# Decoder layer on one core: values of four heads and eight token tiles by seven-for-eight products applied twice, weights fetched in sets through one ring of blocks

## The chip, the cores and the metric

The kernel runs on one core of a Trainium2 chip. The metric is the device time of one execution in microseconds (us). Five engines work side by side, each through its own instructions in order: TensorE (PE, matrix products; PEld is its loading of weights), VectorE (DVE), ScalarE (ACT), GpSimd (POOL) and SyncE (SP, which issues most of the DMAs). An engine waits for another by semaphores. A product is summed in PSUM and must be read out of there by DVE or ACT before its place can be used again.

## What is computed

A decoder layer in float32 over 32 sequences of 64 tokens, width 512: 2048 tokens. The part that matters here is the first block, self-attention with 32 heads of 128 dimensions:

```python
q = (hidden_states @ Wq + bq).reshape(b, n, H, HD)
k = (hidden_states @ Wk + bk).reshape(b, n, H, HD)
v = (hidden_states @ Wv + bv).reshape(b, n, H, HD)
q = rmsnorm(q, gq)
k = rmsnorm(k, gk)
scores = jnp.einsum('bnhd,bmhd->bhnm', q, k) * scale
attn = jax.nn.softmax(scores.astype(jnp.float32), axis=-1).astype(q.dtype)
out = jnp.einsum('bhnm,bmhd->bnhd', attn, v).reshape(b, n, H * HD)
return out @ Wo + bo
...
x = x + _L0_attn_ref(_layernorm(x, axis=-1), ...)
x = x + _L0_xattn_ref(_layernorm(x, axis=-1), ctx_1024, ...)
x = x + _L0_ffn_ref(_layernorm(x, axis=-1), ...)
```

Attention is within a sequence of 64 tokens (b = 32, n = 64). A cross-attention and a mixture of experts follow; the change touches them only through the memory that the attention frees.

## The kernel before, in words

**Tiles.** The 2048 tokens are 16 tiles of 128. The attention runs over the tiles in two halves of eight (`half` 0 and 1), and in each half over 16 groups of two heads (`hg` 0 to 15). One half with one group is called a window here. The eight tiles of a half lie as seven blocks `x1` to `x7` (`halves_x`): the left factors of a seven-for-eight product, in which a 2 x 2 product of matrices is made of seven products of sums of the quarters instead of eight products of the quarters. Such a scheme pays for the product it saves with additions: of the left factors once, of the right factors (the weights), and of the results, which are added to several places when they are read out of PSUM.

**Queries and keys** of windows 1 to 15 use the scheme twice, one inside the other (`Window.outer`, `inner_x`, `Weights.inner`): 49 products of 128 by 128 by 256 (L736) in place of 64. `Window.project` walks four stages n = 0 to 3, which carry outer products (1, 5), (2, 6), (7, 3) and (4) alone. Each stage has four slots m = 0 to 3; stages 0 to 2 have 14 matmuls, stage 3 has 7. Results leave PSUM by `keep` (L747 on DVE, L757 on DVE and L750 on ACT with the bias, in stage 0) and `end` (L760 on DVE). PSUM has three such banks (`ps_a`), and a slot's first product often goes to the bank that the slot before it filled, with `first=False`: it adds to what is there, so it has to wait until `keep` has read that.

**Values** use the scheme once (`HeadGroup.values`, L440): seven steps for each four tiles (a unit, two to a window), each step of four matmuls of 128 by 128 by 128, read out in 128 x 256 pieces by ACT (L456) and DVE (L460). A window has 14 slots in which one value step is put between the products of queries and keys (`Window.v`, and the `plan` in `double`): four in stage 0, three in stage 1, four in stage 2, three in stage 3.

**What else a window carries** is the attention of earlier units: `scale` (POOL L616, ACT L618) at slots (1, 0) and (2, 0), `scores` (L628) and `mix` (L665) at (1, 3) and at the end, the softmax (DVE L281 to L289, ACT L284, POOL L290), the transposition of the probabilities (`turn_probabilities`, L273, L651) at (1, 1) and (3, 2). Within stages 2 and 3, `add` (L816) adds parts of the queries and keys to each other, unit 0 on POOL and unit 1 on DVE, both operands in SBUF; `squares` (ACT L407) squares the results, and at the window's end `sums_of_squares` (L872) sums the squares on PE.

**Weights.** `Weights` holds one group's queries, keys and values in one tile of four blocks of 128 x 2048 (tag "four", two of them). Six DMAs of 256 KB fetch it (L108). POOL makes the sums for the outer scheme (`sums`, L133, four of 128 x 768 a window) and for the inner one (`more_sums`, L163 to L166, four of 128 x 512 and four of 128 x 384).

**Order.** The order on PE, DVE, ACT and POOL within the attention is the program's order (`manual_schedule`); each engine's queue is then run in order. The order of SP's DMAs is chosen by a scheduler. After the attention comes the output projection with `wo` (`wo_sums`, `first_out`, `strassen_out`, L930), and then cross-attention and experts, interleaved.

Of the kernel before, what the change touches and what calls it, by code (L numbers as in the profile page):

```python
# [13 lines left out]
P = 128  # L14
# [4 lines left out]
HG = 2  # L19
# [22 lines left out]
def decoder_layer(  # L42
# [28 lines left out]
    blocks = ctx.enter_context(tc.tile_pool(name="blocks", bufs=7))  # L71
# [11 lines left out]
    def four_blocks(name):  # L83
        four = blocks.tile([P, 4 * BLK], F32, tag="four", name=name, bufs=2)
        return [four[:, bass.ts(i, BLK)] for i in range(4)]
# [5 lines left out]
    class Weights:  # L91
# [3 lines left out]


        def __init__(self, name, hg, queues, between=None):

            self.hg = hg
            all_ = blocks.tile([P, 4 * BLK], F32, tag="four", name=f"w_{name}", bufs=2)  # L100
            n = 2 * W3

            self.w = all_[:, 0 : 4 * n].rearrange(
                "p (k c j h d) -> p k c j h d", k=2, c=2, h=HG, j=3
            )
            for k in range(2):
                for j, src in enumerate((wq, wk, wv)):
                    queues[j].dma_start(  # L108
                        out=self.w[:, k, :, j, :, :].rearrange("p c h d -> p c (h d)"),
                        in_=src[2 * k * P : (2 * k + 2) * P, bass.ts(hg, HW)].rearrange(  # L110
                            "(c p) f -> p c f", p=P
                        ),
                    )
                if between and k == 0:
                    between()
            self.t = all_[:, 4 * n : 7 * n].rearrange("p (i c j d) -> p i c j d", i=3, c=2, j=3)
            b11, b12, b21, b22 = (self.w[:, k, :, :, h, :] for k in range(2) for h in range(HG))
            t1, t2, t4 = (self.t[:, i, :, :, :] for i in range(3))

            self.right = {1: b11, 2: b21, 3: b22, 4: t4, 5: t1, 6: t2, 7: b12}  # L120
            self.more = all_[:, 7 * n : 7 * n + 21 * HD].rearrange(
                "p (i o d) -> p i o d", i=3, o=7
            )
# [7 lines left out]
        def sums(self, engine):  # L131
            def subtract(on, out, a, b):
                on.tensor_tensor(  # L133
                    *(it.rearrange("p c j d -> p (c j) d") for it in (out, a, b)), ALU.subtract
                )

            b11, b12, b21, b22 = (self.w[:, k, :, :, h, :] for k in range(2) for h in range(HG))
            t1, t2, t4 = (self.t[:, i, :, :, :] for i in range(3))
            subtract(engine, t1, b12, b11)
            subtract(engine, t2, b22, t1)  # L140
            yield
            subtract(nc.gpsimd, b12, b22, b12)
            subtract(nc.gpsimd, t4, b21, t2)
            yield

        def more_sums(self):

            for b, of in (
                (self.w.rearrange("p k c j h d -> p c j k h d"), slice(0, 4)),
                (self.t.rearrange("p i c j d -> p c j i d"), slice(4, 7)),  # L150
            ):

                def part(c, j):
                    it = b[:, c, j]
                    return it

                def more(i):
                    it = self.more[:, i, of, :]
                    return it.rearrange("p (k h) d -> p k h d", k=2) if of.start == 0 else it

                b11, b12, b21, b22 = (part(c, j) for c in range(2) for j in range(2))
                t1, t2, t4 = (more(i) for i in range(3))
                nc.gpsimd.tensor_tensor(t1, b12, b11, ALU.subtract)  # L163
                nc.gpsimd.tensor_tensor(t2, b22, t1, ALU.subtract)
                nc.gpsimd.tensor_tensor(t4, b21, t2, ALU.subtract)
                nc.gpsimd.tensor_tensor(b12, b22, b12, ALU.subtract)  # L166
                yield
            self.inner = {}
            for n, o in enumerate((1, 7, 2, 3, 5, 6, 4)):
                r = self.right[o]  # L170
                t1, t2, t4 = (self.more[:, i, n, :] for i in range(3))
                self.inner[o] = {
                    1: r[:, 0, 0, :],
                    2: r[:, 1, 0, :],
                    3: r[:, 1, 1, :],
                    4: t4,
                    5: t1,
                    6: t2,
                    7: r[:, 0, 1, :],
                }  # L180


# [125 lines left out]
    class AttentionInput:  # L308
# [3 lines left out]
        def __init__(self, pair, beside=False, first_alone=False):  # L312

            self.pair = pair
            places = [None, None]
            if beside:
                both = work.tile([P, 2, 2, QT], F32, tag="rsb", name=f"xs{pair}", bufs=2)
                places = [both[:, i, :, :].rearrange("p h n -> p (h n)") for i in range(2)]
            self.xs, self.pt = [], []
            for place in places[0 : 1 if first_alone else 2]:  # L320
                self.load(place)
# [64 lines left out]

    inner_x = {}
# [22 lines left out]
    class HeadGroup:  # L410
# [7 lines left out]
        def __init__(self, hg, quad, w):  # L418
            self.hg, self.quad, self.w, self.name = hg, quad, w, f"{hg}_{quad}"

            self.qk, self.v, self.gains = {}, {}, None
# [9 lines left out]
        def values(self):  # L431


            name, right, left = self.name, self.w.right, quads[self.quad]

            def product(i, to, first=True):

                for j in range(2):
                    for c in range(2):
# [3 lines left out]
                            right[i][:, c, 2, :],  # L443
# [8 lines left out]
            def keep(h, ab, what):  # L452
                self.v[h, ab] = work.tile(
                    [P, 2, HD], F32, tag="v", name=f"v{h}{ab}_{name}", bufs=18
                )
# [247 lines left out]
    class Window:  # L703
# [5 lines left out]
        def __init__(self, units, w, half):  # L709
            self.units, self.w, self.half = units, w, half  # L710
            self.name = f"w{w.hg}_{half}"
            self.values = [it for unit in units for it in [unit.values()] * 7]
# [8 lines left out]
        def v(self):  # L721
            next(self.values.pop(0))
# [5 lines left out]
        def outer(self, os, banks, to, add=None, bias=None):  # L728

            name = f"{os[0]}_{self.name}"  # L730
            n = len(os)
            pa, pb, pc = (it[:, 0:n, :] for it in banks)

            def product(i, bank, first=True):
                for s, o in enumerate(os):
                    nc.tensor.matmul(  # L736
                        bank[:, s, :],
                        self.w.inner[o][i],
# [53 lines left out]
        def project(self, plan):  # L792

            units, hg = self.units, self.w.hg
# [51 lines left out]
            for n, args in enumerate(  # L846
# [10 lines left out]
                for m, _ in enumerate(self.outer(args[0], turned, *args[1:])):  # L857
# [37 lines left out]


# [46 lines left out]
    def wo_sums(b, places):  # L943
# [11 lines left out]
        def make():  # L955
# [10 lines left out]
            for half in range(2):  # L966
                t4.append(block(f"wo_t4{half}").rearrange("p (g f) -> p g f", f=DH))
# [3 lines left out]
        return {1: b11, 2: b21, 3: b22, 4: t4, 5: t1, 6: t2, 7: b12}, make()  # L971
# [516 lines left out]
    b2 = work.tile([2 * NHEAD, HD], F32, tag="v", name="b2", bufs=18)  # L1488
# [7 lines left out]
    coming.extend(AttentionInput(pair, True) for pair in (2, 3))  # L1496
# [97 lines left out]

    groups = [(hg, half) for half in range(2) for hg in range(NHG)]

    def prepare(n):
        if n + 1 < len(groups):
            hg, half = groups[n + 1]
# [305 lines left out]
```

## Time and profile before

| | us |
|---|---|
| median of three runs (1852.62 to 1854.78) | 1854.5 |
| the execution that was profiled | 1854.15 |
| its span, first to last instruction | 1852.4 |
| one window, from stage 0 of one to stage 0 of the next (463.15 to 504.30) | 41.15 |
| from 50 to 1340, about the 30 windows with doubled products | 1290 |
| after 1340: output projection, cross-attention, experts | 512 |

| engine | busy us (share of span) | in the window 463.15 to 504.30 |
|---|---|---|
| PE | 1838.6 (99%) | 41.15 |
| DVE | 1156.5 (62%) | 26.64 |
| ACT | 721.0 (39%) | 19.22 |
| POOL | 860.2 (46%) | 23.51 |

The granted clock of TensorE is 0.999 of full speed. The DMAs moved 165.01 MB; the main queue's packets took 27.8% of the time of the 16 DMA engines. The busy time of PE overlaps at its ends: eight records of L440 have a busy time of 1.05 us, and the next group begins 0.89 us after they began. A float32 matmul of the program is two records in the trace, so the 1470 matmuls of L736 are its 2940 records.

### The profile page before, as it was taken

The numbers are of one execution on the slowest core, as the hardware profiler recorded it, in microseconds if no ns is written. First come the engines' busy times: TensorE is split into PE (matmuls) and PEld (weight loads), VectorE is DVE, ScalarE is ACT, GpSimd is POOL, SyncE is SP. The second block draws the span as 40 slices with busy tenths as digits, with TensorE's granted clock in tenths as the row PEclk, the third lists the DMA queues.
The fourth block names the chain that finished last, engine by engine and source line by source line (L and its number), as shares of the span: only waits on it lengthen the run. The fifth ranks groups of instructions, "written<-read, shape, count | busy, mean of one in ns | idle before, by whom it ended". The sixth has DMA issues, their size and how long they took to land.

```text
span 1852.4 us, 40846 instructions
## 1 busy us (share of the span) xinstructions
PE 1838.6 (99%) x16892; PEld 1605.2 (87%) x16892; DVE 1156.5 (62%) x2044; ACT 721.0 (39%) x1651; POOL 860.2 (46%) x786
## 2 busy tenths in 40 slices
PE   9999999999999999999999999999999999999998
PEld 8889988998899888889888998898888788888876
DVE  7766667676666657666666666666684444544455
ACT  3344445445444443444444444444412112211222
POOL 4855655565556428655556665565132221212120
PEclk9999999999999999999999999999999999999999
DMA  3133323323332232222233222222835221223100
GB/s 127 54 105 99 84 81 93 92 76 88 90 87 73 82 104 70 70 81 70 72 103 87 76 70 70 81 70 73 273 119 183 94 103 61 89 100 110 53 26 24
DMA packets 225099, 165.01 MB, mean 89 GB/s; under 512 B 77776, under 2 KB 204304, under 8 KB 220816
## 3 DMA queue, kind: packets, MB, share of 16 engines
q1 hardware_dynamic: 217808, 156.30, 27.8%
q10 hardware_dynamic: 7104, 6.10, 1.0%
q8 instruction: 133, 2.18, 0.5%
q14 instruction: 54, 0.44, 0.1%
HBM read 121.98 MB, written 40.37 MB: 88 GB/s over the span
## 4 chain that ended last, share of the span: by engine, by line
PE 97%; DVE 2%; DMA 1%; ACT 0%; issue 0%; POOL 0%; SPq 0%; DVEq 0%; POOLq 0%; ACTq 0%
PE p_w L736 35%; PE py L930 21%; PE va L440 12%; PE vb L440 9%; PE s L628 4%; PE o L665 4%; PE ms_w L872 3%; PE pt_p L273 2%; PE pa L498 1%; PE e_x L1159 1%; PE py_x L1175 1%; PE pt_x L273 1%; PE py_x L1170 1%; PE pb L498 1%; PE pm_f L1302 0%; PE pt_f L273 0%
## 5 line engine op out<-in xcount | busy, mean ns | idle before, releaser
L736 PE MATMUL p_w<-x,w 128*128 128x256 f32 x2940 | 720.6, 382 | 2.2 <-DVE qk L747 1.5
L736 PEld LDWEIGHTS p_w<-x,w 128*128 128x128 f32 x2940 | 521.5, 190 | 58.2 <-issue 2.0
L747 DVE TENSOR_TENSOR qk<-p_w,qk 128x512 f32<-128x512 f32 x360 | 212.9, 599 | 145.1 <-PE p_w L736 144.0
L760 DVE TENSOR_TENSOR qk<-p_w,qk 128x512 f32<-128x512 f32 x360 | 222.2, 623 | 101.7 <-PE p_w L736 98.4
L290 POOL TENSOR_TENSOR prob<-prob,inv 128x512 f32<-128x512 f32 x64 | 72.4, 1131 | 454.7 <-PE va L440 237.4
L440 PEld LDWEIGHTS va<-w,x 128*128 128x128 f32 x2048 | 268.5, 192 | 13.0
L440 PE MATMUL va<-w,x 128*128 128x128 f32 x2048 | 269.9, 275 | 0.0
L456 ACT COPY v<-va 128x256 f32<-128x256 f32 x256 | 96.6, 377 | 401.9 <-PE va L440 401.9
L407 ACT ACTIVATE sq<-qk 128x512 f32<-128x512 f32 x256 | 161.3, 631 | 176.4 <-DVE qk L760 57.8
L133 POOL TENSOR_TENSOR w<-w 128x768 f32<-128x768 f32 x124 | 225.0, 1825 | 9.2 <-DMA w<-in_wv_dram 6.9
L930 PE MATMUL py<-wo,a 128*128 128x256 f32 x992 | 227.0, 382 | 0.0
L930 PEld LDWEIGHTS py<-wo,a 128*128 128x128 f32 x992 | 183.8, 190 | 33.4 <-issue 8.9
L440 PEld LDWEIGHTS vb<-w,x 128*128 128x128 f32 x1536 | 201.4, 192 | 9.7
L440 PE MATMUL vb<-w,x 128*128 128x128 f32 x1536 | 202.4, 275 | 0.0
L930 PE MATMUL py<-wo_t,a 128*128 128x256 f32 x672 | 154.9, 381 | 0.0
L930 PEld LDWEIGHTS py<-wo_t,a 128*128 128x128 f32 x672 | 124.7, 190 | 18.9 <-issue 2.4
L1054 POOL TENSOR_TENSOR x<-x,p 128x256 f32<-128x256 f32 x42 | 40.7, 988 | 164.2 <-ACT p L1107 73.9
L460 DVE TENSOR_TENSOR v<-vb,v 128x256 f32<-128x256 f32 x192 | 81.0, 422 | 49.0 <-PE vb L440 27.9
L816 POOL TENSOR_TENSOR qk<-qk 128x256 f32<-128x256 f32 x120 | 90.7, 756 | 28.0 <-DVE qk L760 23.3
L680 ACT ACTIVATE ot<-o,bvt 128x256 f32<-128x256 f32 x256 | 99.4, 469 | 2.2 <-PE o L665 2.2
L281 DVE TENSOR_TENSOR prob<-s,g_w 128x512 f32<-128x512 f32 x60 | 41.5, 691 | 85.9 <-PE s L628 81.3
L284 ACT ACTIVATE prob<-prob 128x512 f32<-128x512 f32 x64 | 40.4, 631 | 128.7 <-DVE prob L283 128.7
(254 smaller groups left out, 2290.3 us busy)
## 6 DMA issues: line engine op xcount, KB each, us to landing
mixed<-ot SPq DMA_DIRECT2D x64, 512.0 KB
a<-mixed SPq DMA_DIRECT2D x32, 1024.0 KB
w<-in_wq_dram SPq DMA_DIRECT2D x64, 256.0 KB
w<-in_wk_dram SPq DMA_DIRECT2D x62, 256.0 KB
w<-in_wv_dram SPq DMA_DIRECT2D x62, 256.0 KB
g_w<-row_w SPq DMA_DIRECT2D x120, 128.0 KB
x<-in_x_dram SPq DMA_DIRECT2D x20, 256.0 KB
wo<-in_wo_dram SPq DMA_DIRECT2D x4, 1024.0 KB
```

The source lines that it names most:

```text
L133: on.tensor_tensor(*(it.rearrange("p c j d -> p (c j) d") for it in (out, a, b)), ALU.subtract)
L407: nc.scalar.activation(sq, of, AF.Square)
L440: nc.tensor.matmul(to[:, j, :], left[i][:, c, j, :], right[i][:, c, 2, :], start=first and j == 0 and c == 0, stop=c == 1, skip_group_chec ...
L456: nc.scalar.copy(self.v[h, ab], what)
L460: nc.vector.tensor_tensor(it, what, it, ALU.add)
L628: nc.tensor.matmul(s[h * SEQ : (h + 1) * SEQ, i, b, :], qk[:, 0, tok], qk[:, 1, tok], start=True, stop=True,)
L680: nc.scalar.activation(ot[:, h, :, b * SEQ : (b + 1) * SEQ], o[b][:, h, :, :], AF.Identity, bias=bvt[:, hg * HG + h : hg * HG + h + 1],)
L736: nc.tensor.matmul(bank[:, s, :], self.w.inner[o][i], inner_x[self.half, o][i], start=first and s == 0, stop=True, skip_group_check=True,)
L747: nc.vector.tensor_tensor(to(t, j), bank, add(t, j), ALU.add)
L760: nc.vector.tensor_tensor(to(t, j), bank, to(t, j), ALU.add)
L816: on.tensor_tensor(to, to, what, ALU.add)
L930: nc.tensor.matmul(py, a[:, g, :], b[g // KH][:, g % KH, :], start=n == 0 and g == 0, stop=n == last and g == NHG - 1,)
```

## The change

Windows 0 and 1 of each half make their values as before. From window 2 on, the values of two windows (four heads) and of all eight tiles of the half are made together, by seven-for-eight products applied twice (`ValueGroup`): 49 products of 128 by 128 by 256, each as two matmuls of 128 columns, 98 matmuls for two windows where there were 112. They form 25 steps in four sets: 14 steps in the even window's slots, 11 in the odd window's, whose last three slots (stage 3) have none. A step of sets 0 to 2 has four matmuls as before, and its result is 128 x 512 for each read-out; set 3's steps have four matmuls for two products (one in the last), and its read-outs are 128 x 256. In set 0, four of seven read-outs are copies on ACT, all others are additions on DVE. Set 2 adds eight `join` additions of 128 x 256 with both operands in SBUF, four on POOL (tiles t = 0) and four on DVE (t = 1).

The weights come as `WeightSet`s, one for each stage, four for the queries and keys of a window and four for the values of two windows. Each takes one block of a single ring of 13 blocks, which also holds the seven blocks of the half's tiles; the ring of seven and the two tiles of four blocks go. Sets 2 and 3 fetch one column half of the weights again instead of reading it from sets 0 and 1. POOL makes one or two sums of 128 x 512 for the outer scheme of a set (`outer_sums`) and four of 128 x 256 (in set 3 of 128 x 128) for the inner one (`inner_sums`).

The first windows' `Weights` take four blocks of the ring, and 12 DMAs in place of six. `wo`'s first loads move from the start of the last window to slots (1, 0) and (2, 0). One sum of `wo` (`wo_t4`) lies in a buffer of the attention and is made a second time behind it (`make_again`). Some buffers change their tag.

```diff
-    blocks = ctx.enter_context(tc.tile_pool(name="blocks", bufs=7))
+    blocks = ctx.enter_context(tc.tile_pool(name="blocks", bufs=13))
...
     def four_blocks(name):
-        four = blocks.tile([P, 4 * BLK], F32, tag="four", name=name, bufs=2)
-        return [four[:, bass.ts(i, BLK)] for i in range(4)]
+        return [block(f"{name}{i}") for i in range(4)]
...
+    class WeightSet:
+        def __init__(self, n, name, sources, width, base):
+            self.n = n
+            it = block(f"ws{n}_{name}")
+            self.raw = it[:, 0 : 8 * HD].rearrange("p (o c f) -> p o c f", o=2, c=2)
+            self.more = it[:, 8 * HD : 16 * HD].rearrange("p (e o d) -> p e o d", e=4, o=2)
+            for j, src in enumerate(sources):
+                to = self.raw[:, :, :, j * width : (j + 1) * width]
+                if n < 2:
+                    for c in range(2):
+                        nc.sync.dma_start(
+                            out=to[:, :, c],
+                            in_=src[bass.ts(2 * n + c, P), base : base + 2 * width].rearrange(
+                                "p (o f) -> p o f", o=2
+                            ),
+                        )
+                else:
+                    base_ = base + (width if n == 2 else 0)
+                    nc.sync.dma_start(
+                        out=to.rearrange("p o c f -> p (o c) f"),
+                        in_=src[:, base_ : base_ + width].rearrange("(k p) f -> p k f", p=P),
+                    )
+            self.slots = slice(1, 2) if n == 3 else slice(0, 2)
+
+        def outer_sums(self, before):
...
+            a, b = (self.raw[:, o] for o in range(2))
+            if self.n == 0:
+                subtract(b, b, a)
+            elif self.n == 1:
+                subtract(b, b, before.raw[:, 1])
+            elif self.n == 2:
+                subtract(a, b, a)
+            else:
+                subtract(b, b, before.raw[:, 0])
+                subtract(b, b, a)
+
+        def inner_sums(self, part):
...
+            for out, a, b in ((t1, b12, b11), (t2, b22, t1), (t4, b21, t2), (t7, b22, b12))[
+                2 * part : 2 * part + 2
+            ]:
+                nc.gpsimd.tensor_tensor(out, a, b, ALU.subtract)
...
+    class ValueGroup:
...
+        def outer(self, n, os, to, add):
...
+            def product(i, bank, first=True):
+                for s, o in enumerate(os):
+                    x = inner_x[self.half, o][i]
+                    for t in range(2):
+                        nc.tensor.matmul(
+                            bank[:, s, bass.ts(t, HD)],
+                            x[:, bass.ts(t, HD)],
+                            right[s][i],
+                            start=first and s == 0 and t == 0,
+                            stop=True,
+                            skip_group_check=True,
+                        )
+
+            def keep(bank, t, j):
+                if add is None:
+                    nc.scalar.copy(to(t, j), bank)
+                else:
+                    nc.vector.tensor_tensor(to(t, j), bank, add(t, j), ALU.add)
+
+            def end(bank, t, j):
+                nc.vector.tensor_tensor(to(t, j), bank, to(t, j), ALU.add)
+
+            def join(t, j):
+                if n == 2:
+                    on = nc.vector if t else nc.gpsimd
...
+                    on.tensor_tensor(p2, p2, p3, ALU.add)
+                    on.tensor_tensor(p3, p3, p1, ALU.add)
+
+            short = n == 3
+            product(1, pa)
+            keep(pa, 0, 0)
+            if not short:
+                yield
+            product(2, pb)
+            end(pb, 0, 0)
+            join(0, 0)
+            yield
...
-                (0, 3): [lambda n=n: sums_of_next(n), lambda: make(1)],
-                (1, 0): [lambda: make(1)],
-                (1, 3): [lambda: make(1)],
-                (3, 0): [lambda: make(2)],
...
+            places = [(n, k) for k in range(4)] + [(n + 1, k) for k in range(2)]
+            for k in range(4):
+                for at in places[k + 2 if (hg, k) != (1, 0) else 1 : k + 3]:
+                    if at[0] == n or hg < NHG - 1:
+                        also(k, 0, lambda at=at: load_qk(*at))
+                at = places[k + 1]
+                if at[0] == n or hg < NHG - 1:
+                    also(k, 1, lambda at=at: sums_of(qk_sets, *at))
+                    also(k, 2, lambda at=at: qk_sets[at].inner_sums(1))
+            for k in range(2):
+                at = (half, hg // 2, 2 * (hg % 2) + k + 1)
+                if at[2] == 4:
+                    at = (half, at[1] + 1, 0)
+                if 0 < at[1] < NHG // 2:
+                    also(2 * k, 0, lambda at=at: load_v(*at))
+                    also(2 * k, 3, lambda at=at: sums_of(v_sets, *at))
+                    also(2 * k + 1, 1, lambda at=at: v_sets[at].inner_sums(1))
...
+            if hg == 1:
+                values = [it for unit in units for it in [unit.values()] * 7]
+            elif hg % 2 == 0:
+                steps = group.steps()
+                values = [steps] * 14
+            else:
+                values = [steps] * 11
+            double(Window(units, n, half, values), more)
...
+    make_again()
```

## The prediction

> **What bounds the kernel now.** First the page: busy times and slices.
>
> ```profile
> span 1852.4 us, 40846 instructions
> PE 1838.6 (99%) x16892; PEld 1605.2 (87%) x16892; DVE 1156.5 (62%) x2044; ACT 721.0 (39%) x1651; POOL 860.2 (46%) x786
> ...
> DVE  7766667676666657666666666666684444544455
> ...
> POOL 4855655565556428655556665565132221212120
> ```
>
> PE never rests, and DVE and POOL have 30 to 45% left in the first 28 slices, which are the attention. That is a mean; the change loads particular stages. So next, the busy time in stretches: one whole window, then stages 2 and 3 of the window before it (columns: us; PE, PEld, DVE, ACT, POOL busy; clock; DMA share; GB/s).
>
> ```profile
> 463.15:504.30 41.15, 41.15 (x449) 36.93 (x443) 26.64 (x47) 19.22 (x38) 23.51 (x20) 1.00 0.28 79
> 443.16:452.88 9.72, 9.72 (x66) 9.00 (x61) 7.53 (x14) 4.40 (x9) 5.05 (x7) 1.00 0.18 56
> 452.88:459.11 6.23, 6.23 (x44) 5.59 (x42) 5.27 (x11) 3.52 (x7) 4.22 (x4) 1.00 0.02 4
> ```
>
> DVE is busy 12.8 of the 15.95 us of these two stages (80%): the room there is 3.2 us, not 14. Third, the timeline, for prices: PE's slots, then DVE beside POOL in stage 3.
>
> ```profile
> 406.48 1.05 PE L440 MATMUL vb<-w,x 128*128 128x128 f32 x8
> 407.37 1.89 PE L736 MATMUL p_w<-x,w 128*128 128x256 f32 x8
> 409.10 1.05 PE L440 MATMUL va<-w,x 128*128 128x128 f32 x8
> 409.99 1.03 PE L736 MATMUL p_w<-x,w 128*128 128x256 f32 x4
> 410.85 1.05 PE L440 MATMUL vb<-w,x 128*128 128x128 f32 x8
> ```
>
> From start to start a value step takes 0.89 us (407.37 - 406.48), a slot's products 1.73 us in stages 0 to 2 and 0.86 in stage 3.
>
> ```profile
> 493.94 0.41 DVE L816 TENSOR_TENSOR qk<-qk 128x256 f32<-128x256 f32 x1
> ...
> 495.29 1.00 POOL L164 TENSOR_TENSOR w<-w 128x384 f32<-128x384 f32 x1
> 495.59 0.98 DVE L816 TENSOR_TENSOR qk<-qk 128x256 f32<-128x256 f32 x1
> 496.37 1.06 POOL L165 TENSOR_TENSOR w<-w 128x384 f32<-128x384 f32 x1
> ...
> 496.83 0.74 DVE L747 TENSOR_TENSOR qk<-p_w,qk 128x256 f32<-128x256 f32 x2
> 497.39 0.99 POOL L166 TENSOR_TENSOR w<-w 128x384 f32<-128x384 f32 x1
> 497.49 1.18 DVE L816 TENSOR_TENSOR qk<-qk 128x256 f32<-128x256 f32 x1
> ```
>
> The same addition of two SBUF operands takes 0.41 us alone and 0.98 or 1.18 beside POOL: each ends about 0.3 us after the POOL instruction that was running when it began. Over its 120 instances (page: 85.2 us) the mean is 0.71. Two PSUM read-outs in a row take 0.74 together, so the second costs 0.33.
>
> **What the change removes on PE.** 14 fewer value matmuls in each of 14 pairs of windows: 196. At 0.886 / 4 = 0.2215 us each that is 43.4 us, or 3.1 a pair. By steps: the even window keeps 14 full steps, so its 41.14 us; the odd one has 7 full and 7 half steps, 41.14 - 12.40 + 9.30 = 38.04 us. The whole saving is in the odd window, and in its stage 3 no value step is left between the products.
>
> **What it adds on DVE.** Prices: 128 x 512 from PSUM 0.64 in a row (443.69 to 444.33, L283 then L747; 0.69 for one alone), 128 x 256 0.33, a softmax operation that depends on the one before 0.72. An addition with both operands in SBUF costs c. The odd window's stages 1 to 3: queries and keys 7 x 0.64 + 7 x 0.64 + 7 x 0.33 = 11.27; values, three read-outs of set 2 and seven of set 3, 1.92 + 2.31 = 4.23; softmax 3 x 0.72 + 0.89 = 3.05; four joins and four additions L816, 8c. Together D = 18.55 + 8c. PE's own work from stage 1 to the end of the sums of squares: 7 x 0.866 + 3 x 0.886 + 0.44 + 2.17 = 11.33 (the 0.44 a transposition, the 2.17 scores and mixture), then 7 x 0.866 + 7 x 0.443 = 9.16, then 7 x 0.433 + 0.44 = 3.47, then 1.86: 25.82.
>
> DVE's queue is tied to PE's at both ends: it can begin 1.07 us after stage 1 (a product and the 0.2 us to the read-out), it waits about 0.2 us for PE in six places (1.2), and behind its last read-out come ACT's square, 0.63, and the last of the sums of squares, some 0.35. So the stretch lasts at least D + 3.25, and PE stalls D - 22.6 = 8c - 4.0. At c = 0.41 that is nothing, at the mean of 0.71 it is 1.7, at the longest row (1.19) 5.5. I take c from POOL's load. Now POOL is busy 57% of a window and c is 0.41 + 0.30, so a busy POOL costs 0.53; at 90%, worked out next, c = 0.41 + 0.9 x 0.53 = 0.89, and the stall is 3.1 us. It eats the saving.
>
> The place where it is felt: a slot's first product adds to a bank that `keep` of the slot before must have read (L747). The value step between gave `keep` 0.89 us. In stage 3 of the odd window it is gone, so two products of 0.43 us stand between a product and the next on its bank, against 0.2 + 0.42 and what is queued before it on DVE: L816, joins, value read-outs. Behind a late L816 wait ACT's squares, and behind them PE's sums of squares.
>
> The even window: stages 2 and 3 get seven value read-outs of 0.64 where DVE had three of 0.42, +3.2, and four L816 at 0.89 instead of 0.75, +0.6, on 12.8: 16.6 against 15.95. I take 0.7 us of stall (0 if slack in the banks holds it, 1.5 if each lateness meets PE).
>
> **What it adds on POOL.** Prices: 128 x 512 1.28 (L163), 128 x 256 0.73 (L816 on POOL, its median), 128 x 128 0.46 by the same slope. A window's four sets of queries and keys: 5 x 1.28 + 12 x 0.73 + 4 x 0.46 = 17.0; values half of as much, 8.5; additions 2.9, gains and softmax 4.2: 32.6 us in the even window and, with four joins, 35.5 in the odd one, against 23.5 now. That is 79% and 93% of 41.14 and 38.04. [...] I add nothing for POOL on top (0 to 3 us a pair): its late weight sums are due a stage later, about three slots of 2.6 us.
>
> [...]
>
> **DMA and SP.** A window's weights grow from 1.5 to 3 MB (sets 2 and 3 fetch a column half again) and rows from 1 KB to 512 B for queries and keys. Weights are 1.5 of 79 GB/s x 41.15 us = 3.25 MB, so 0.13 of the 0.28 DMA share. Priced by bytes the share becomes 0.41, by packets (1536 to some 5000) about 0.58: hidden either way. SP issues about 15 weight DMAs a window, not 6, at 0.46 us: 6.9 us of 41. Each waits for a block of the ring; 13 less 7 leaves six, and behind it on SP stand the rows that the gains come from. The list of the built program has the loads one to two stages ahead of their sums, so I price this wait at nothing; if that cover fails, see the last rival.
>
> **Small terms.** At the start ACT issues eight weight DMAs instead of four before its first layernorm operation, which now begins (5.28) just as the last issue ends (5.18): 4 x 0.45 = +1.8. In windows 3, 5, 7, 9 of half 0 a normalization (0.6 us on DVE) falls in stage 1 of the odd window: +2.4 (0 if hidden). `make_again`, two DVE operations of about 2.28 us, is covered by a DVE that is 40 to 50% busy after 1340; without that cover +4.6. `wo`'s later loads have three stages left: nothing; one late stage would be 10.
>
> **Sum.** A pair: -3.1 + 3.1 + 0.7 = +0.7; 14 pairs +10; with 1.8 and 2.4: +14 on the profiled 1854.15 gives 1868. That execution lies 0.35 below the median, inside the runs' spread of 2.2, so I leave it. Within 0.2% (3.7 us) a measurement cannot tell a change here.
>
> **The rivals.**
> 1. *PE stays the bound, faster.* c stays at 0.71 and slack in the banks holds the even windows: -3.1 + 1.7 = -1.4 a pair, -20 + 4: 1838; with no stall at all, 1811 + 4. For it: the trace has no PE wait above 2.2 us in all of L736, though DVE is 80% full there. Against it: DVE's sums above and the rows beside POOL. Range 1811 to 1850.
> 2. *No change*: stalls a little under my sum, 1851 to 1858.
> 3. *Late weights, slower.* From the point where a set's load waits for its ring block until less than a stage (10 us) is left, POOL's queue stands at the first sum for the DMA, and PE after it. Now such a wait (POOL L133, 6.9 us in three) is 2.3 us; one in each of 28 windows gives 64, so 1920. Against it: loads come early in the list.
>
> **How the numbers follow.** My case 0.57, rival 1 0.30, rival 2 0.05, rival 3 0.08. Faster 0.30, same 0.05, slower 0.65. My case alone spans 1858 (c = 0.8) to 1905 (c about 1.1, even windows 1.1 late: -3.1 + 4.8 + 1.1 = +2.8 a pair, 39 + 4 = 1897, and some POOL on top). The range cuts the lower part of rival 1 and the top of my case and rival 3: 1828 to 1905.
>
> **What would show it.** Right: value matmuls 1372 plus 224 for 1792; even windows near 42 us and odd ones near 41 to 42, not 38; PE idle before the products of stages 2 and 3 and the sums of squares, released by DVE's read-outs and ACT's squares; DVE near 30 us a window, POOL above 32, and the two-SBUF additions near 0.9. Wrong: odd windows of 38 to 39 us with PE as full as now (rival 1), or PE and POOL idle behind weight DMAs (rival 3).

## The result and the profile after

The changed kernel takes 1885.68 us (median of four, 1885.16 to 1886.6) against 1854.64 of the kernel before in the same session: ratio 1.0167, 95% interval 1.0149 to 1.0184. It is 31 us slower; the forecast was 13.4 us slower. The profiled execution has a span of 1884.9 us against 1852.4, so 32.5 us are to be found in it. First the page of the changed kernel: busy times, then the chain of waits by engine, then three groups (columns as in the prediction's page: busy us, mean ns, idle before, what ended it).

```profile
span 1884.9 us, 41677 instructions
PE 1831.8 (97%) x16500; PEld 1569.0 (83%) x16500; DVE 1298.2 (69%) x2270; ACT 664.9 (35%) x1483; POOL 1170.1 (62%) x1414
...
PE 77%; POOL 11%; DVE 9%; issue 3%; DMA 0%; ACT 0%; POOLq 0%; SPq 0%; DVEq 0%; ACTq 0%
...
L768 PE MATMUL p_w<-x,ws_q 128*128 128x256 f32 x2940 | 731.9, 386 | 34.2 <-POOL ws_q L199 20.0
...
L437 ACT ACTIVATE sq<-qk 128x512 f32<-128x512 f32 x256 | 157.5, 629 | 362.6 <-POOL qk L848 219.3
...
L318 POOL TENSOR_TENSOR prob<-prob,inv 128x512 f32<-128x512 f32 x64 | 72.3, 1129 | 209.0 <-DVE inv L317 143.0
```

PE has 392 records fewer (196 matmuls), but the chain that ended last, 97% PE before, now runs 11% through POOL and 9% through DVE. The products (L768) waited 20.0 us for POOL's inner weight sums (L199). POOL itself is busy only 62%, and its softmax multiplication (L318) was preceded by 209 us of idle POOL, 143 of them ended by DVE's reciprocal (L317). POOL idles and is waited for at once; that points at the order of its work rather than at its amount, which e5 tests.

Next an even and an odd window (columns: us; PE, PEld, DVE, ACT, POOL busy; clock; DMA share; GB/s).

```profile
439.37:480.96 41.59, 41.52 (x449) 37.06 (x443) 30.09 (x51) 18.44 (x34) 33.30 (x41) 1.00 0.41 115
480.96:522.68 41.72, 39.59 (x421) 33.67 (x415) 33.71 (x59) 15.98 (x30) 35.51 (x44) 1.00 0.42 116
```

Both are longer than the 41.15 of before (41.14 between sums of squares); the odd one should have lost 3.1 us of PE work, and its PE is busy 1.9 us less than the even one's, but it stands. Its PE pauses, and beside them POOL's queue in the same stretch (timelines: start, duration, then the idle time before and its releaser in brackets):

```profile
512.15 0.71 PE L978 MATMUL va<-ws_v,x 128*128 128x128 f32 x4 [0.31 <-DVE v L994]
...
514.25 1.13 PE L768 MATMUL p_w<-x,ws_q 128*128 128x256 f32 x4 [0.18 <-POOL ws_q L199]
516.63 1.13 PE L768 MATMUL p_w<-x,ws_q 128*128 128x256 f32 x4 [1.25 <-POOL ws_q L199]
```

```profile
503.25 1.86 POOL L199 TENSOR_TENSOR ws_q<-ws_q 128x256 f32<-128x256 f32 x2
506.72 1.04 POOL L318 TENSOR_TENSOR prob<-prob,inv 128x512 f32<-128x512 f32 x1 [1.61 <-ACT ot L710]
507.72 1.04 POOL L646 TENSOR_TENSOR g_w<-g_w,rq 128x512 f32<-128x512 f32 x1
508.72 1.53 POOL L848 TENSOR_TENSOR qk<-qk 128x256 f32<-128x256 f32 x2
510.21 1.27 POOL L175 TENSOR_TENSOR ws_q<-ws_q,ws_q 128x512 f32<-128x512 f32 x1
511.55 1.33 POOL L175 TENSOR_TENSOR ws_q<-ws_q 128x512 f32<-128x512 f32 x1
512.97 1.24 POOL L199 TENSOR_TENSOR ws_q<-ws_q 128x128 f32<-128x128 f32 x2
514.16 1.59 POOL L848 TENSOR_TENSOR qk<-qk 128x256 f32<-128x256 f32 x2
515.72 0.86 POOL L199 TENSOR_TENSOR ws_q<-ws_q 128x128 f32<-128x128 f32 x2
```

POOL stops at 505.11 with the multiplication at the head of its queue. Behind it stand the gains (L646), the additions (L848) and the sums of set 3 (L175, L199), whose last ends at 516.58; PE's product starts at 516.63. The odd row names ACT's L710 as the releaser, which ended at 506.70; DVE's reciprocal (L317), which the multiplication reads, had ended at 506.55, so without L710 it would have stood there only 0.15 us less. Set 3's weights are not the reason: SP had issued their last fetch by 477.98, and POOL's sums of them begin at 510.21 without a wait for a DMA. In the even window the same head waits longer:

```profile
464.24 1.04 POOL L318 TENSOR_TENSOR prob<-prob,inv 128x512 f32<-128x512 f32 x1 [6.53 <-DVE inv L317]
```

Taking the period from one window's sums of squares to the next gives the whole account (us of span, changed minus before):

| place | forecast | measured |
|---|---|---|
| start, to the first sums of squares | +1.8 | +6.4 |
| the first doubled window (hg = 1) of each half | 0 | +2.9 and +3.3 |
| 14 pairs of windows (even 41.67, odd 41.64) | +10 | +14.7 |
| normalizations beside odd windows 3, 5, 7, 9 of half 0 (42.5) | +2.4 | +3.5 |
| single units | 0 | -0.3 |
| everything behind the last window | 0 | +2.0 |
| sum | +14 | +32.5 |

The first doubled windows have the longest pauses of PE in the windows. It waits there for parts of the left factors (`x`, L426) that POOL makes behind set 3's sums, and works on at a clock of 0.50 (last section), so that eight matmuls of L473 took 1.77 us, not 1.05:

```profile
777.13 1.13 PE L768 MATMUL p_w<-x,ws_q 128*128 128x256 f32 x4 [2.18 <-POOL x L426]
778.10 1.77 PE L473 MATMUL va<-wv,x 128*128 128x128 f32 x8
```

What the 2.0 us behind the last window are isn't settled; e5 gets 0.8 of them back.

### The profile page after: what moved, and what is told of

It is laid out like the page before. It is cut to its first block, busy times and chain, and to the rows that moved or that the text cites. A ratio compares the mean times of both kernels' runs of the same rounds, so it can differ in the third digit from the quotient of the medians.

```text
span 1884.9 us, 41677 instructions
## 1 busy us (share of the span) xinstructions
PE 1831.8 (97%) x16500; PEld 1569.0 (83%) x16500; DVE 1298.2 (69%) x2270; ACT 664.9 (35%) x1483; POOL 1170.1 (62%) x1414
## 4 chain that ended last, share of the span: by engine, by line
PE 77%; POOL 11%; DVE 9%; issue 3%; DMA 0%; ACT 0%; POOLq 0%; SPq 0%; DVEq 0%; ACTq 0%
PE p_w L768 24%; PE py L1070 21%; PE va L978 6%; POOL ws_q L175 4%; PE vb L978 4%; PE s L658 4%; POOL qk L848 3%; PE ms_w L904 3%; PE o L695 3%; DVE qk L779 3%; POOL ws_q L199 2%; PE pa L528 2%; POOL g_w L646 2%; PE va L473 1%; PE pt_p L301 1%
## 5 line engine op out<-in xcount | busy, mean ns | idle before, releaser
L768 PE MATMUL p_w<-x,ws_q 128*128 128x256 f32 x2940 | 731.9, 386 | 34.2 <-POOL ws_q L199 20.0
L768 PEld LDWEIGHTS p_w<-x,ws_q 128*128 128x128 f32 x2940 | 521.9, 191 | 113.1 <-POOL ws_q L199 31.3
L199 POOL TENSOR_TENSOR ws_q<-ws_q 128x256 f32<-128x256 f32 x480 | 337.1, 712 | 21.0
L437 ACT ACTIVATE sq<-qk 128x512 f32<-128x512 f32 x256 | 157.5, 629 | 362.6 <-POOL qk L848 219.3
L779 DVE TENSOR_TENSOR qk<-p_w,qk 128x512 f32<-128x512 f32 x360 | 210.6, 596 | 83.6 <-PE p_w L768 72.8
L978 PEld LDWEIGHTS va<-ws_v,x 128*128 128x128 f32 x1568 | 209.0, 191 | 21.0 <-DVE v L994 10.0
L978 PE MATMUL va<-ws_v,x 128*128 128x128 f32 x1568 | 212.6, 276 | 4.4 <-DVE v L994 4.4
L318 POOL TENSOR_TENSOR prob<-prob,inv 128x512 f32<-128x512 f32 x64 | 72.3, 1129 | 209.0 <-DVE inv L317 143.0
L978 PEld LDWEIGHTS vb<-ws_v,x 128*128 128x128 f32 x1176 | 154.5, 192 | 6.5
L978 PE MATMUL vb<-ws_v,x 128*128 128x128 f32 x1176 | 158.5, 275 | 0.0
L199 POOL TENSOR_TENSOR ws_v<-ws_v 128x256 f32<-128x256 f32 (+1 forms) x224 | 147.4, 668 | 8.8
L175 POOL TENSOR_TENSOR ws_q<-ws_q 128x512 f32<-128x512 f32 x90 | 116.8, 1298 | 2.4
L710 ACT ACTIVATE ot<-o,bvt 128x256 f32<-128x256 f32 x256 | 99.2, 469 | 2.2 <-PE o L695 2.2
L848 POOL TENSOR_TENSOR qk<-qk 128x256 f32<-128x256 f32 x120 | 89.1, 742 | 5.3 <-DVE qk L792 0.6
```

Source lines behind the costliest of these rows:

```text
L175: nc.gpsimd.tensor_tensor(*(it.rearrange("p c f -> p (c f)") for it in (out, a, b)), ALU.subtract)
L199: nc.gpsimd.tensor_tensor(out, a, b, ALU.subtract)
L318: nc.gpsimd.tensor_tensor(prob, prob, _bc(inv, k), ALU.mult)
L437: nc.scalar.activation(sq, of, AF.Square)
L710: nc.scalar.activation(ot[:, h, :, b * SEQ : (b + 1) * SEQ], o[b][:, h, :, :], AF.Identity, bias=bvt[:, hg * HG + h : hg * HG + h + 1],)
L768: nc.tensor.matmul(bank[:, s, :], right[s][i], inner_x[self.half, o][i], start=first and s == 0, stop=True, skip_group_check=True,)
```

## The experiments

All edits are made on the changed kernel unless said otherwise. e1 to e9 were run once each, e11 four times, e10 and e12 ten times; the kernel before took 1852.6 to 1857.7 us beside them, so small differences between single runs are read from the windows, which agree much more closely (the 14 doubled windows behind the first of half 0 take 584.80 us in the changed kernel and 584.85 in e3). The letters in the expectations: P is POOL's order (something early in its queue waits, and weight sums stand behind it), D is VectorE's load as the prediction had it, C the amount of POOL's work wherever it stands, S the start. An edit shifts the lines below it: L850 in e1 and e11 is L848 of the changed kernel, L770 is L768, L781 is L779.

**e1_late: the multiplication later in POOL's queue.**

```diff
         nc.vector.reciprocal(inv, sums)
+        yield
         nc.gpsimd.tensor_tensor(prob, prob, _bc(inv, k), ALU.mult)
...
-            waiting.append(lambda: next(it, None))
+            step = lambda: next(it, None)
+            waiting.extend([step] + [lambda: None] * 3 + [step])
```

> The changed kernel, with the softmax's multiplication on POOL issued about two slots later, behind the additions L848 and the first sums of the next weight set; nothing else is changed. POOL's order (theory P): POOL stands at that multiplication until DVE's reciprocal is there, 6.5 us in the even window and 1.6 in the odd one, while set 3's sums that PE needs next wait behind it. Then the even window falls from 41.59 to 41.1 to 41.2 us, the odd one from 41.72 to 39.5 to 40.5, the whole to 1855 to 1870. DVE's load (theory D, the prediction's): the odd window is set by DVE's read-outs and two-SBUF additions; then the even window stays, the odd one falls by 0.3 at most, and the whole stays above 1880.

1948.14 us: 62 us worse, windows of 42.5 to 46.2 us. Neither theory expected longer windows. POOL's timeline of an even window:

```profile
485.31 1.54 POOL L850 TENSOR_TENSOR qk<-qk 128x256 f32<-128x256 f32 x2 [9.69 <-DVE qk L794]
```

and PE's in the same window:

```profile
494.41 1.13 PE L770 MATMUL p_w<-x,ws_q 128*128 128x256 f32 x4 [1.09 <-POOL ws_q L199]
```

With the multiplication out of the way the additions came to the head, and they wait for DVE even longer (9.69 us), with set 3's sums still behind them. The multiplication itself now runs from 492.31, still ahead of set 3's last two sums, which end at 494.36; at the end of the odd window before, PE waited 2.43 us for the same sums. In the whole run PE's waits for L199 grew from 20.0 to 51.9 us, those for L779 (here L781) from 6.7 to 19.3, and the granted clock was 0.50 for 58 us in place of 17. So it need not be the multiplication that waits: whatever waits ahead of set 3's sums holds them up. The edit was the wrong remedy; the reading P survives in that wider form, which e5 tests.

**e2_nojoin: without DVE's four joins.** It leaves out the joins of tiles t = 1, so those values are incomplete.

```diff
-                if n == 2:
+                if n == 2 and not t:
```

> The changed kernel without the four joins of each odd window on DVE (tiles t = 1 of value set 2), so half of the values lack two of their terms. D: 4 x about 0.8 us of DVE go from stage 1 of the odd window; it falls by 2 to 3 us to 39 to 39.7, the whole by 28 to 42 us. P: only the stall at slot (1, 2) (0.46) and some 0.6 us ahead of the softmax go: the odd window falls by 0.5 to 1.1 us, the whole by 7 to 15.

1869.23 us. Odd windows 41.64 to 40.76 in half 1 (-0.9), 42.5 to 40.75 in half 0; even ones unchanged at 41.67. D asked for 2 to 3 us, P for 0.5 to 1.1 (and 7 to 15 us in all, where 16.5 came): the joins aren't where most of the time is, though the four odd windows of half 0 that carry the normalizations on DVE are helped most.

**e3_start: two of three queues of the first weights on SP, as many DMAs on ACT as before.**

```diff
-        "0_0", 0, (nc.sync, nc.scalar, nc.scalar), lambda
+        "0_0", 0, (nc.sync, nc.sync, nc.scalar), lambda
```

> The changed kernel with the first window's four key-weight DMAs issued by SP instead of ACT, so ACT issues four weight DMAs, as many as before the change. Theory S: the start is 6.4 us later because ACT's first layernorm operation (9.64 instead of 5.28 us) stands behind eight DMA issues that wait for earlier DMAs, and PE then starts at a halved clock; the first sums of squares come at 31 to 33 us instead of 36.96, the whole falls by 4 to 6 us, all else stays. Rival: the weights themselves land later, in rows of 512 B; then it falls by 1 us at most.

1880.45 us, 5.2 less than the changed kernel. The first sums of squares come at 31.96 us, not 36.96 (before: 30.57; 35.9 in e4 and e5, which keep the changed kernel's start). ACT's first layernorm operation and PE's first transpositions, first in the changed kernel, then in e3:

```profile
9.64 0.30 ACT L284 ACTIVATE rs_a<-mv_a,ln_eps 128x2 f32<-128x2 f32 x1 [7.43 <-DMA w<-in_wk_dram]
...
10.81 1.97 PE L301 MATMUL pt_a<-ident,x 128*128 128x128 f32 x8 [3.47 <-DVE x L331]
```

```profile
5.43 0.30 ACT L284 ACTIVATE rs_a<-mv_a,ln_eps 128x2 f32<-128x2 f32 x1 [3.22 <-DVE mv_a L278]
...
6.60 1.11 PE L301 MATMUL pt_a<-ident,x 128*128 128x128 f32 x8
```

ACT was held until 9.64 (before: 5.28), 4.4 us longer and not 4 x 0.45: its eight weight issues stood apart, the last ended at 9.54, and the trace's releaser is a weight transfer, at a time when the DMA engines are full (share 1.00 from 2 to 7 us). The clock, 0.50 for 6.8 us, added to the delay (last section).

**e4_ring: the ring and the weight sets alone, values once seven-for-eight as before** (`ValueWeights` for every window in place of the values' sets).

```diff
-            if hg == 1:
+            if hg > 0:
                 values = [it for unit in units for it in [unit.values()] * 7]
```

> Part of the change alone: the ring of blocks and the weight sets for queries and keys stay, but the values of all windows are made as in the first ones (seven products once, 112 matmuls for two windows, one block of value weights per window). PE has its 43.4 us back, DVE's and POOL's value work is as before the change. D: no DVE overload, so windows of 41.14 us and the whole at 1868 to 1872 (the start's 6.4 and the first windows' 6.2 stay). P: the blocked POOL still delays set 3's sums: windows of 41.4 to 41.6 us, the whole at 1876 to 1884.

1903.41 us, 42.46 us in every window: worse than the whole change, and both theories were too low. So the half of the change that saves nothing on PE costs 1.3 us a window as it is ordered here (e12 mends the order). Where PE and ACT wait (two timelines of e4):

```profile
433.61 1.16 PE L473 MATMUL va<-wv,x 128*128 128x128 f32 x8 [0.72 <-ACT v L486]
```

```profile
431.80 0.63 ACT L437 ACTIVATE sq<-qk 128x512 f32<-128x512 f32 x1 [3.23 <-POOL qk L848]
```

A second path from POOL to PE: ACT stands at a square that waits for POOL's late addition, and the copy of a value bank (L486) that PE needs is behind it in ACT's queue.

**e5_set3: set 3's sums earlier on POOL**, from slots (2, 1) and (2, 2) to (1, 2) and (1, 3), ahead of the multiplication and the additions. Nothing is left out.

```diff
-                    also(k, 1, lambda at=at: sums_of(qk_sets, *at))
-                    also(k, 2, lambda at=at: qk_sets[at].inner_sums(1))
+                    here = {0: ((0, 1), (0, 2)), 1: ((1, 1), (1, 2)),
+                            2: ((1, 2), (1, 3)), 3: ((3, 1), (3, 2))}[k]
+                    also(*here[0], lambda at=at: sums_of(qk_sets, *at))
+                    also(*here[1], lambda at=at: qk_sets[at].inner_sums(1))
```

> The changed kernel with the sums of set 3 (queries and keys) moved ahead on POOL, from slots (2, 1) and (2, 2) to (1, 2) and (1, 3): before the softmax's multiplication and before both pairs of additions L848, into the time in which POOL stands idle. Order on POOL (P): PE's waits for POOL sums in stage 3 go (0.3 in the even window, 1.4 in the odd one), and the additions of unit 0 no longer wait behind 3.8 us of sums; even window 41.1 to 41.2 us, odd one 40.0 to 41.2, whole 1866 to 1878. POOL's capacity (C: 35.5 us of work and its waits fill the odd window in any order): the odd window stays at 41.7, even 41.2, whole 1879 to 1882.

1858.06 us, where P had 1866 to 1878: 27.6 of the 31 us are gone, by moving six POOL instructions a window (4.5 us of work) and changing none. About 1 us of it is at the start, which the edit doesn't touch. POOL's queue in an odd window of e5, then PE's in the same:

```profile
831.58 1.27 POOL L175 TENSOR_TENSOR ws_q<-ws_q,ws_q 128x512 f32<-128x512 f32 x1
832.92 1.28 POOL L175 TENSOR_TENSOR ws_q<-ws_q 128x512 f32<-128x512 f32 x1
834.28 1.94 POOL L199 TENSOR_TENSOR ws_q<-ws_q 128x128 f32<-128x128 f32 x4
836.18 1.05 POOL L318 TENSOR_TENSOR prob<-prob,inv 128x512 f32<-128x512 f32 x1
837.18 1.05 POOL L646 TENSOR_TENSOR g_w<-g_w,rq 128x512 f32<-128x512 f32 x1
838.18 3.39 POOL L848 TENSOR_TENSOR qk<-qk 128x256 f32<-128x256 f32 x4
```

```profile
838.90 0.71 PE L978 MATMUL va<-ws_v,x 128*128 128x128 f32 x4 [0.57 <-DVE v L994]
...
840.90 1.13 PE L768 MATMUL p_w<-x,ws_q 128*128 128x256 f32 x4 [0.43 <-DVE qk L779]
842.25 1.13 PE L768 MATMUL p_w<-x,ws_q 128*128 128x256 f32 x4 [0.21 <-DVE qk L779]
```

The sums fill the time in which POOL had stood idle, and the multiplication finds its operand ready: no bracket is left on POOL. All PE waits on POOL have gone from the doubled windows too, those on L426 among them; what remains is DVE's. Windows: even 41.32, odd 40.88 (41.05 beside normalizations), the first of each half 40.41 and 40.47 instead of 43.89 and 44.89 (before: 40.97 and 41.59). C is refuted: the work is the same and the time isn't.

**e6_sums: sets 1 and 2 one slot earlier as well** (0: (0, 0), (0, 1); 1: (1, 0), (1, 1)).

> As e5_set3, and the sums of sets 1 and 2 one slot earlier too, so that POOL works on them in stage 0 while it now waits for DVE's read-outs ahead of the joins (1.9 us in the odd window). P: odd window 0.5 to 1.5 us below e5_set3, even 41.14. C: as e5_set3.

1855.9 us. Odd windows 40.46 in half 1 (0.4 below e5, P had 0.5 to 1.5), but 41.62 beside the normalizations, where e5 had 41.05. So the best place differs between the two kinds of window.

**e7_act: e5 with the multiplication on ACT** (eight scalings of 64 columns in place of one POOL instruction).

> As e5_set3, with the softmax's multiplication on ACT, as eight scalings of 128 x 64, instead of POOL; ACT is busy 16 to 18 us of a window. C: POOL loses 2.1 us of 35.5 a window, so the odd window falls by 1 to 2 us against e5_set3. P: the multiplication is no longer in POOL's way, but set 3's sums are already ahead of it: 0 to 0.5 us. If eight small operations cost ACT more than 2 us or it stands waiting for the reciprocal with copies behind it, windows become longer.

1860.17 us; odd 40.77, even 41.38. With the order mended, taking 1.05 us off POOL twice a window brings nothing. That is a second answer against C.

**e8_nojoin5: e5 without DVE's joins** (the edit of e2; those values are incomplete).

> e5_set3 without the joins of tiles t = 1 on DVE (half of the values lack two terms). D: with POOL's order out of the way DVE's load is what is left, and 3.3 us of it go: the odd window falls by 1.5 to 2.5 us against e5_set3. P or C: by 0.9 or less, as it did in e2_nojoin.

1852.13 us; odd 40.43 (-0.45), even unchanged. Four additions cost 0.45 us a window, not the 1.5 to 2.5 of D.

**e9_gaps and e11_front: where the odd window's eleven steps of values stand.** In e9 (on e5) three slots of stages 0 to 2 go without a step, so that stage 3 gets three. In e11 (on e10) two slots at the front take two, and one sum of the values' weights moves a slot ahead for it.

```diff
-                values = [steps] * 11
+                values = [None if i in (2, 5, 9) else steps for i in range(14)]
```

> The kernel with the sums of set 3 early (e5), and in odd windows the eleven steps of values are spread: the third, sixth and tenth slot go without one, so that the bare products of stage 3 get three steps between them. Nothing else is changed. Theory L (latency: in the last stage, which has one pair of blocks fewer and no step of values between its products, PE stands for DVE's read-out of the bank just filled): odd windows shorten from 40.88 us to 39.3 to 40.3, fourteen of them, time 1838 to 1851. Theory D (capacity: DVE has too much to do in an odd window, wherever the steps stand): odd windows stay at 40.7 to 41.1, time 1855 to 1861. Even windows stay at 41.3 in both.

> On top of e10: in odd windows the eleven steps of values stand earlier (two each in the first two slots, one in the next seven, none in stage 2's last two slots and in stage 3; the last inner sum of the values' fourth set one slot earlier for that). Spreading them late (e9) made an odd window 1.7 us longer. Theory D local (VectorE is full in stages 2 and 3, where the additions of the seven-for-eight products stand, and each step of values put there delays a read-out that PE waits for): taking two steps out of stage 2 shortens an odd window from 40.48 to 39.5 to 40.2, sixteen of them, time 1838 to 1846. Theory L (what is left is the latency of bare products, and e9 lost its time for another reason): more bare products, odd windows 40.6 to 41.5, time 1852 to 1867. Even windows stay at 41.3.

Both are worse: 1879.87 us (odd windows 42.6, 42.9 beside normalizations) and 1876.41 us (41.9 to 43.9; ratio to before 1.0118, 1.0094 to 1.0142). Later steps add value read-outs and joins to stages 2 and 3 of a full DVE (busy 15.5 of the last 16.6 us of an odd window in e9); this answers against L, which expected a gain from it, and against D, which expected no change. Earlier steps leave more bare products there: D local, which expected a gain, missed, and the loss goes L's way but beyond its 41.5. In stage 3 of e11, PE's timeline and then DVE's:

```profile
933.81 1.13 PE L770 MATMUL p_w<-x,ws_q 128*128 128x256 f32 x4 [0.97 <-DVE qk L781]
935.91 1.13 PE L770 MATMUL p_w<-x,ws_q 128*128 128x256 f32 x4 [0.97 <-DVE qk L781]
```

```profile
934.20 1.32 DVE L850 TENSOR_TENSOR qk<-qk 128x256 f32<-128x256 f32 x1
935.44 0.74 DVE L781 TENSOR_TENSOR qk<-p_w,qk 128x256 f32<-128x256 f32 x2
```

An addition of 1.32 us stands on DVE ahead of the read-out that PE waits for. Moving steps shifts such meetings; no rule for the best place came out of the two runs, and how latency and DVE's load share what is left isn't settled.

**e10_both: e3 and the early sums together** (e6's places, e5's beside the normalizations).

> The two largest places mended together: the first weights on two SP queues (as in e3), and the sums early (all three sets where no normalization runs, as in e6; set 3 alone beside the normalizations, as in e5). If the two are independent: 5.2 us from the start, 27.6 from set 3's place and about 3 from the other sets in 20 windows, so 1885.7 - 35.8 = 1850, bounds 1847 to 1853, just ahead of the kernel before (1854.6; ratio 0.9975). If the start's gain is taken up by the first windows, 1855.

1850.48 us, ratio to before 0.9981 (0.9972 to 0.9991): 35.2 us from the changed kernel, so the two mendings add up, and the change with them is ahead of the kernel before by some 4 us, or 0.2%. Even windows 41.32, odd 40.48 (41.05 beside normalizations). Not all of this lead is the pairs': in the profiled executions (1848.7 and 1852.4) they give 2.9 us, the first doubled windows and the single units between the halves 3.9, and start and end take 3.1 back.

**e12_ringmend: e4 with both mendings.**

> The ring and the sums by sets with the values once seven-for-eight as before (as in e4, 1903.4 us, 42.46 us a window), now with the two mendings of e10 (first weights on two SP queues; sums early). Theory P (in e4 too the ring's loss was the place of set 3's sums on POOL, with ACT's squares and the copies of values behind POOL's late additions): windows 41.1 to 41.5, time 1849 to 1862, and then the values' part alone, e10 against this, is worth only 0 to 10 us. Rival R (the ring costs in itself when ACT's copies of values wait behind squares, wherever the sums stand): windows 42.0 to 42.5, time 1878 to 1895, and the values' part is worth some 30 to 45 us.

1853.42 us, ratio 0.9992 (0.9982 to 1.0001), against e4's 1903.41. Chain of waits and products of e12:

```profile
PE 97%; DVE 1%; DMA 1%; ACT 0%; issue 0%; SPq 0%; POOL 0%; ACTq 0%; DVEq 0%; POOLq 0%
...
L768 PE MATMUL p_w<-x,ws_q 128*128 128x256 f32 x2940 | 720.5, 382 | 0.8 <-DVE qk L779 0.6
```

Nearly all its doubled windows last 41.14 us, as before the change, though POOL does 108 us more work in the kernel (968.7 against 860.2). The ring, the sets and their doubled fetches cost nothing in these windows; R is refuted. And the values applied twice are worth 2 to 3 us in all (e10 against e12; 2.9 in the pairs' windows), not 43: an odd window gains 0.66 (beside a normalization 0.1), an even one loses 0.18. The gain in the first windows and between the halves isn't theirs: e12 has it as well.

## Why the prediction was right and wrong

The direction held, and so did the argument that the matmuls saved aren't the time saved; rivals 1 and 2 fell. But the direction held by something that the prediction had put at nothing: with POOL's order and the start mended the same change takes 1850.48 us, at the meeting of rivals 1 and 2. Rival 3 fell too: no PE pause in the windows is ended by a weight DMA, and the DMA share came out at 0.41 as priced by bytes.

**The step that failed** is "I add nothing for POOL on top (0 to 3 us a pair): its late weight sums are due a stage later, about three slots of 2.6 us". The load under it was right: 32.6 and 35.5 us of POOL work forecast, 33.30 and 35.51 measured. But lateness was judged by the slot in which the sums are issued, and that cover is counted from when POOL gets to them. POOL gets to them behind a multiplication that waits for DVE's softmax, and behind additions that wait for DVE's read-outs. e5 prices this place at some 27 of the 31 us: about 1.1 us a pair, all of the 6.2 us of the first windows, most of the normalizations' share, 1.9 us of the single unit behind the last window of half 0 and 0.8 behind the last window of all. A pair's share lies within the bounds given (0 to 3); taking the lower bound for nothing lost it, and hg = 1, where the values still come the old way but the sets' sums already run, was never looked at.

**The start** was the right mechanism, mis-sized: 1.8 forecast, 6.4 measured, 5.0 of which e3 gets back. Only the issues' own time was counted. They also stood behind transfers (the last issue ended at 9.54, before the change at 5.18), and after PE's pause of 3.47 us the clock was 0.50 for 6.8 us.

**VectorE's term** was too large, and that a pair came out near its forecast (0.7 against 1.05 measured) is luck: two errors met. Of the 3.8 us a pair that the prediction gave to VectorE, 2.6 are measured once POOL's order is mended (2.4 and 0.18, below), so a pair is then 0.5 us shorter than before, not 0.7 longer; POOL's order, put at nothing, made up for that. The additions that c stands for, in the changed kernel, by form:

```profile
L848 DVE TENSOR_TENSOR qk<-qk 128x256 f32<-128x256 f32 x120 | 70.5, 587 | 0.0
...
L1005 DVE TENSOR_TENSOR v<-v 128x256 f32<-128x256 f32 x28 | 30.9, 1105 | 1.0
...
L1004 DVE TENSOR_TENSOR v<-v 128x256 f32<-128x256 f32 x28 | 13.8, 495 | 1.0
```

Together 115.2 us over 176: c = 0.65, not 0.89. By the prediction's 8c - 4.0 the odd stall would be 1.2 us. With POOL mended (e10, where c is 0.70 and the sum would give 1.6) it is 40.48 - 38.04 = 2.4, against 3.1 forecast, and the even one's 0.18 against 0.7. So most of the saving is still lost with POOL out of the way, and nearly all the PE waits of e10's doubled windows for which the trace names a releaser are for DVE (14.4 of the some 36 us lost in 14 pairs; for the rest it names nobody). But it doesn't go as a sum over three stages: dropping four additions, worth 3.2 us of DVE time by the rows above, returns 0.45 (e8). The rows of e11 point to single meetings, each an addition ahead of a read-out; no run shows that these are all.

Single additions are long beside POOL (1.32 in e11; the second join's mean of 1.11), but the mean of 0.65 at 80 to 85% POOL load, against 0.71 at 57% before the change, says that c did not grow with POOL's load as the prediction assumed. The upper end of its range takes c as about 1.1 and an odd stall of 4.8 us: no run shows that, and what the changed kernel showed in its place is the mean of 0.65, with 1.11 in the second joins alone and 0.50 in the first.

## What to carry to other kernels

Price an in-order engine by its queue, not by its busy share: for each instruction that another engine will need, list what stands ahead of it and what that waits for. Work whose inputs come early (weight sums) belongs ahead of work whose inputs come late (the last step of a softmax), even if it is needed later. Before judging a change's idea, run its carrying structure alone and its order mended: here the idea was worth 2 to 3 us and one place in a queue some 27.

## What the hardware showed that was not expected

The granted clock fell in the first microseconds of the changed kernel, and three times more before its last microsecond. Stretches of the first time (columns as above; the clock is the last but two):

```profile
10.00:10.50 0.50, 0.00 (x0) 0.00 (x0) 0.29 (x1) 0.17 (x1) 0.00 (x0) 0.74 0.92 299
...
11.00:14.00 3.00, 3.00 (x14) 2.55 (x14) 1.75 (x5) 1.80 (x7) 0.00 (x0) 0.50 0.87 275
...
17.00:17.50 0.50, 0.50 (x5) 0.47 (x4) 0.10 (x1) 0.00 (x0) 0.00 (x0) 0.93 0.90 252
```

PE idled 3.47 us up to 10.81, and the clock was 0.50 from about 10.24 (0.74 in the first row means that about half of it ran at 0.50) to 17.07, for 6.8 us: eight transpositions took 1.97 us instead of 1.11. The four groups of PE work that ran in this time took 2.9 us longer than the same four of the kernel before, on top of the pause.

The other three times the clock was 0.50 for 3.41 us, from 95.57, 692.90 and 778.24 us on: soon after PE pauses of 2.35, 2.67 and 2.18 us, in the first doubled windows and between the halves. How long a pause it takes isn't shown. These beginnings lie 85.33, 682.66 and 768.00 us behind the first one (10.24): 25, 200 and 225 times 3.413 us, the length of one such stretch, as on a fixed grid, and the pauses fill 2.0 to 2.9 us of the step of that grid before each of the four. The kernel before has one such stretch between the halves (from 673.24), e5 one at its start, and e10 and e12 none up to their last 5 us. So a part of what e5 gave back in the first windows is clock: a wait for POOL of some 2 us there cost more than its own length.
